# One shared score tile, head banks that alternate, and score products made half a step early in a decoder's joint stage

## The chip, the core and the metric

The kernel runs on one core of one Trainium2 chip. The metric is device time in microseconds (us), lower is better. The core has engines that run side by side, each with its own queue of instructions in a fixed order: PE (matrix products and, with an identity, transposes), DVE (vectors), ACT (activations such as exp), POOL (vectors too), and SP, which here starts transfers (DMA). They signal each other through semaphores. An instruction that waits holds up all that stands behind it on its engine. PE writes its products to PSUM, an on-chip memory[...], from which DVE and ACT read.

## The reference

Two decoder layers, each of self-attention, cross-attention and a feed-forward part, with a layer norm after each residual. The change lies in layer 0's cross-attention and the feed-forward part after it. Cut to these:

```python
x = _layernorm(x + _L0_attn_ref(x, ...))
x = _layernorm(x + _L0_xattn_ref(x, ctx_2048, ...))      # 16 heads of 16, 2048 rows, 2048 keys
x = _layernorm(x + _L0_ffn_ref(x, ...))
...
# in _L0_xattn_ref:
q = _fq_sym(q, axis=-1); k = _fq_sym(k, axis=-1); v = _fq_sym(v, axis=2)   # rounded to 8 bits
attn = softmax(einsum('bhqd,bhkd->bhqk', q, k))
attn = _fq_unsigned(attn, axis=-1)                                        # 0..255 per row
out = einsum('bhqk,bhkd->bhqd', attn, v)
# in _L0_ffn_ref:
h = silu(gate) * up
out = einsum('bsi,hi->bsh', h, w_down)
```

## The kernel before

The 2048 rows are 16 tiles of 128. Layer 0's cross-attention and its feed-forward part form one joint stage, from about 878 to 1875 us, in which the feed-forward work of earlier rows is laid between the attention work of later ones. It is a loop over 128 steps `(gp, i, u)`: eight groups `gp` of two row tiles, in each eight pairs of heads `i`, in each the two row tiles `u`. So a group is 16 steps. A step handles two heads (`hh` 0 and 1) of one row tile against all 2048 keys.

A step has two halves (`part`) of 1024 keys. In each half:

- `scores` (L781) makes four products on PE of 128 rows by 512 keys: for c = 0 and 1 (512 keys each), one per head. The two heads use the upper and lower 64 rows of the array. Each head's two products go to a tile `s` of two PSUM banks. The pool keeps two such tiles, so each half reuses the tiles of the half before.
- `scaled` (L794) makes one DVE pass per head, which scales the 1024 scores into `e` and carries the row's running maximum. Below, S1 is the pass of head 0 and S2 that of head 1.
- `words_T` (L829) transposes on PE the 8-bit weights of an earlier step (four products); `words_out` (L835) copies them out of PSUM, on DVE in the first half and on ACT in the second.
- `context` (L847) multiplies 8-bit weights by values, ten or twelve small products a half in three halves of four. They are split in two parts by `hh`.
- `weights8` (L813) is ACT's exponential over 2048 keys for one head of the step before, straight to 8 bits. At the end of a step `exponent` (L809) negates the maximum for it.
- `spread` (L841) is POOL's cast that puts the weights in the order `context` wants.

The order on PE, DVE, ACT and POOL is that in which the code records the instructions (`manual_schedule`); nothing reorders them. Besides the attention, `unit` (L1057) makes a gate or an up product of the feed-forward part (two products of 128 by 256), twice in eight of a group's 16 steps, and starts the load of a coming weight block on SP. `pair_work` (L1064), at the end of each half, makes the queries of later tiles, the attention's output product, the feed-forward part's down product and the transposes around them. `later` and `due` put off the DVE, ACT and POOL sides of these to named places of following halves.

In the first group there is no feed-forward work, in the second only gate and up products. After the last step a tail finishes the last rows: `ffn_gate` with tag "s" takes the two score tiles in turn for eight gate and up pairs, while ACT reads the tile of the pair before (`ffn_out`), and `ffn_down_psum` takes one for the down product.

PE's order in one half of before: four score products; transposes; put-off PE work; in the second half the unit; both parts of the contexts; then `pair_work`, which holds the first half's unit.

Of the kernel before, what the change touches and what calls it, by code (L numbers as in the profile page):

```python
# [18 lines left out]
F32 = mybir.dt.float32  # L19
# [8 lines left out]
P = 128  # L28
# [4 lines left out]
G = 512  # L33
# [15 lines left out]
def decoder(ctx: ExitStack, tc: tile.TileContext, w: dict, out: bass.AP):  # L49
    nc = tc.nc  # L50
# [538 lines left out]
    with ExitStack() as ph:  # L589
# [188 lines left out]
            ssum = stat.tile([P, 2, 16], F32, tag="ssum", name="ssum", bufs=3)  # L778
            groups[gp] = ([], ssum)

        def scores(gp, i, u, half, st):  # L781

            t = 2 * gp + u
            s = [ps.tile([P, 2, G], F32, tag="s", name="s", bufs=2) for _ in range(2)]
            for c in range(2):
                at = (2 * half + c) * G
                for hh in range(2):
                    r = slice(64 * hh, 64 * hh + 64)
                    nc.tensor.matmul(  # L789
                        s[hh][:, c, :], lhsT=qT[t % 4][r, i, :], rhs=kT[r, i, at : at + G], start=True, stop=True  # L790
                    )
            return s

        def scaled(gp, i, u, half, hh, st, s):  # L794

            nc.vector.tensor_scalar(  # L796
                st["e"][hh][:, half, :],
                s[hh].rearrange("p a b -> p (a b)"),
                qs[2 * gp + u][:, 2 * i + hh : 2 * i + hh + 1],
                None if half == 0 else st["mx"][:, 0, hh : hh + 1],  # L800
                ALU.mult,
                ALU.max,
                accum_out=st["mx"][:, half, hh : hh + 1],
            )
# [24 lines left out]
        def words_T(hh, st):  # L829
            pt = ps.tile([P, 4, P], F32, tag="tp", name="aTp", bufs=2)  # L830
            for b in range(4):
                nc.tensor.transpose(pt[:, b, :], st["a"][hh][:, b * P : (b + 1) * P], ident)  # L832
            return pt

        def words_out(hh, st, pt, copy):  # L835

            at = wk.tile([P, 4, P], F32, tag="at", name="at", bufs=3)
            copy(at.bitcast(U16), pt.bitcast(U16))  # L838
            st["at"][hh] = at
# [75 lines left out]
        def ffn_gate(q, i, n, tag="misc"):  # L915

            if n == 0:
                pp = ps.tile([P, 2, G] if tag == "s" else [P, 2, 2 * P], F32, tag=tag, name="gu", bufs=2 if tag == "s" else 1)
                ffn_ps[q] = pp[:, 0].rearrange("p (n c) -> p n c", n=2) if tag == "s" else pp
            at = slice((q % 2) * 2 * P, (q % 2) * 2 * P + 2 * P)  # L920
            wt = wgu[i, n]
            for k in range(2):
                nc.tensor.matmul(  # L923
                    ffn_ps[q][:, n, :], lhsT=wt[:, k, :], rhs=xT[q // 2][:, k, at], start=k == 0, stop=k == 1
                )
# [23 lines left out]
            eng.tensor_tensor(hs[q][:, i], th, gu[:, 0], ALU.mult)  # L949

        def ffn_down_psum(tag="misc"):
            pp = ps.tile([P, 2, G] if tag == "s" else [P, G], F32, tag=tag, name="pd", bufs=2 if tag == "s" else 1)
            return (pp[:, 0] if tag == "s" else pp).rearrange("p (u d) -> p u d", u=2)

        def ffn_down(q, js, pd):
            for j in js:
# [100 lines left out]
        def unit(n, k, at):  # L1057

            gp, r = n // 16, n % 16
            q = gp - 1 if r >= 8 else gp - 2  # L1060
            if r in units and 0 <= q < LAST:
                ffn_half(q, units[r], k, at)
# [52 lines left out]
        with tc.manual_schedule(engines=set(ordered)):  # L1115
            for n in range(len(steps) + 9):
                now = steps[n] if n < len(steps) else None
                if now is not None:
                    if n % 16 == 0:
                        group(n // 16)  # L1120
                    if n < NB:
                        nc.gpsimd.tensor_tensor(xs[n], xs[n], bp, ALU.add)
                    states[n] = {
                        "e": [wk.tile([P, 2, 2 * G], F32, tag="e", name="e", bufs=4) for _ in range(2)],
                        "mx": stat.tile([P, 2, 2], F32, tag="smx", name="smx"),
                        "a": [],
                        "at": {},
                    }
                for part in range(2):
                    at = 2 * n + part  # L1130
                    if now is not None:
                        s = scores(*now, part, states[n])
                        for hh in range(2):
                            scaled(*now, part, hh, states[n], s)
                    due(at, "DVE")

                    m = n - 2 + part
                    if 0 <= m < len(steps):
                        pt = words_T(1 - part, states[m])
                        words_out(1 - part, states[m], pt, nc.scalar.copy if part else nc.vector.tensor_copy)  # L1140
                    due(at, "PE")
                    if part == 1:
                        unit(n, 1, at)
                    for hh in range(2):

                        q = n - 3 if (n - 3) % 2 == 1 else n - 4
                        turn = (2 * (n - q) + part, hh)
                        if 0 <= q < len(steps) and turn in turns:
                            gp, i, _ = steps[q]
                            if turn == (7, 0) and i % 4 == 0:  # L1150
                                os[gp, i // 4] = ps.tile([P, 2 * P], F32, tag="o", name="o")
                            o = os[gp, i // 4]
                            context(i, range(*turns[turn]), aTs[gp, i], o)
                            if turn == (9, 1):
                                aTs.pop((gp, i))
                                if i % 4 == 3:
                                    later(
                                        at + 1,
                                        "ACT first",
                                        nc.scalar.copy,  # L1160
                                        ot[:, i // 4],
                                        os.pop((gp, i // 4)).rearrange("p (u q) -> p u q", u=2),
                                    )
                                if i == 7 and gp < LAST:
                                    later(at, "DVE last", sums, gp)
                                    for u in range(2):
                                        later(at + 1, "POOL", by_dim, gp, u)
                    due(at, "ACT first")

                    if 0 <= n - 1 < len(steps):  # L1170
                        weights8(*steps[n - 1], part, states[n - 1])
                    due(at, "ACT")
                    if 0 <= n - 2 < len(steps):
                        gp, i, u = steps[n - 2]
                        if part == 0 and u == 0:
                            aTs[gp, i] = wk.tile([P, NB, 2, 2 * P], BF16, tag="aT", name="aT")
                        due(at, "POOL first")
                        spread(u, part, states[n - 2], aTs[gp, i])
                    due(at, "POOL first")
                    due(at, "POOL")  # L1180
                    if now is not None and part == 1:
                        exponent(states[n])
                    due(at, "DVE last")
                    if (n, part) == (len(steps), 1):
                        later(at + 1, "DVE", sums, LAST)
                        for u in range(2):
                            later(at + 2, "POOL", by_dim, LAST, u)
                    if n < len(steps):
                        pair_work(n, bool(part))
                    else:  # L1190
                        tail_work(n, bool(part))
                if n == len(steps) + 3:
                    ffn_load_all()
                states.pop(n - 3, None)
            assert not put_off, put_off

            for i in range(NI):
                for n in range(2):
                    ffn_gate(LAST, i, n, "s")
                th, gu = ffn_tiles(LAST, i, tail=True)  # L1200
                ffn_out(LAST, th, gu)
                ffn_sigmoid(th, nc.vector)
                ffn_mult(LAST, i, th, gu, nc.vector)
            exp_tables()
            for u in range(2):
                ffn_put_out(LAST, range(NI * u, NI * u + NI), 0, "s")
                due(1, "DVE")
            due(1, "POOL")
            due(2, "POOL first")
# [498 lines left out]
```

## Time and profile before

| | |
|---|---|
| median of three runs | 2923.34 us (2921.56 to 2929.32) |
| the profiled execution, and its span | 2931.01 us, 2929.3 us |
| mean granted PE clock | 0.951 of full speed |
| busy over the span: PE, DVE, ACT, POOL | 2617.0, 1985.8, 1583.3, 1238.2 us |
| joint stage: first to last score pass | 879.6 to 1815.7 us |
| eight groups of it | 108.5, 112.9, 116.7, 119.5, 119.5, 119.5, 119.5, 120.1 us |
| busy 1340 to 1460: PE, DVE, ACT, POOL | 97.06, 97.91, 93.79, 83.95 of 120 us |

A line of a group of the profile has the source line, the engine and operation, the tile written and the tile read, shapes and count, then busy time in us and the mean of one in ns, and last the engine's idle time ahead of it and what ended most of that. A line of the timeline has the start and the length in us, engine, line, operation, tiles and count of records; brackets hold the idle time before it and who ended it. PE's 32-bit products appear as two records each. PEld is the loading of weights to PE. The granted clock is the share of full speed that PE was given.

### The profile page before, as it was taken

Reading aid. Unit: us, or ns where it says so; the run is one execution under the profiler, and the core shown is the slowest. Engines: PE = TensorE matmul, PEld = TensorE weight load, DVE = VectorE, ACT = ScalarE, POOL = GpSimd, SP = SyncE. Lnnn points to the kernel's source line nnn. Section 1 sums busy time; section 2 is a strip of 40 time slices with the busy share of each in tenths; the row PEclk is TensorE's granted clock in tenths of the full one; section 3 lists DMA queues with packets and bytes.
Section 4 is the critical chain, followed back from the end, with each engine's and each line's share of the span. In section 5 each row is a group of like instructions: output and inputs, shape, how many; then the busy total and the mean of one; then the engine's idle time right before and its main releaser. Section 6 shows DMA issues by size and latency. Waiting matters only on the chain. (4 is left out here: it accounts for less than half of the span.)

```text
span 2929.3 us, 43541 instructions
## 1 busy us (share of the span) xinstructions
PE 2617.0 (89%) x15989; PEld 1629.2 (56%) x16020; DVE 1985.8 (68%) x4501; ACT 1583.3 (54%) x2858; POOL 1238.2 (42%) x1390
## 2 busy tenths in 40 slices
PE   6999999999977778888787888899988899999998
PEld 3677777777743344444444444566655554655646
DVE  5677878777668888878878876377777764233232
ACT  3455555555536887878778777255555443122120
POOL 5544444444365666767768667322322210000000
PEclk9999999999986899989989898899999999999999
DMA  8000000000010000100000001310010012021110
GB/s 234 1 1 1 1 1 1 1 1 1 1 41 5 1 17 14 30 12 19 23 12 26 12 19 27 110 58 2 2 46 12 7 26 73 29 62 40 47 58 15
DMA packets 84997, 79.61 MB, mean 27 GB/s; under 512 B 19728, under 2 KB 66288, under 8 KB 84272
## 3 DMA queue, kind: packets, MB, share of 16 engines
q1 hardware_dynamic: 83520, 73.41, 8.2%
q0 software_dynamic: 1264, 3.42, 0.5%
q8 instruction: 126, 2.06, 0.3%
q14 instruction: 87, 0.71, 0.1%
HBM read 74.57 MB, written 2.23 MB: 26 GB/s over the span
## 5 line engine op out<-in xcount | busy, mean ns | idle before, releaser
L842 POOL CAST aT<-at 128x2048 bf16<-128x2048 uint8 x256 | 482.9, 1891 | 253.6 <-DVE at L838 221.4
L820 ACT ACTIVATE a<-e,snl 128x2048 uint8<-128x2048 f32 x256 | 513.4, 2005 | 2.8
L796 DVE TENSOR_SCALAR_CACHE_REDUCE e<-s,qs 128x1024 f32<-128x1024 f32 x256 | 319.0, 1282 | 123.9 <-PE s L789 110.6
L796 DVE TENSOR_SCALAR_CACHE_REDUCE e<-s,qs,smx 128x1024 f32<-128x1024 f32 x256 | 333.7, 1341 | 44.8 <-PE s L789 42.7
L832 PE MATMUL aTp<-ident,a 128*128 128x128 f32 x1024 | 191.5, 316 | 103.5 <-ACT a L820 103.1
L789 PE MATMUL s<-kT,qT 64*128 64x512 bf16 x1024 | 221.4, 427 | 49.2 <-DVE e L796 45.0
L832 PEld LDWEIGHTS aTp<-ident,a 128*128 128x128 f32 x1024 | 122.8, 156 | 243.1 <-ACT a L820 210.8
L838 ACT COPY at<-aTp 128x1024 uint16<-128x1024 uint16 x128 | 129.5, 1012 | 199.4 <-PE aTp L832 182.2
L1620 DVE TENSOR_TENSOR h<-h,up 128x512 f32<-128x512 f32 (+1 forms) x100 | 68.8, 688 | 192.6 <-PE up L1616 191.3
L1619 ACT ACTIVATE h<-gate 128x512 f32<-128x512 f32 (+1 forms) x100 | 59.7, 597 | 220.4 <-PE gate L1616 220.2
L1616 PE MATMUL gate<-xT,w_L_ffn_w1g 128*128 128x512 f32 x352 | 167.7, 595 | 0.0
L1616 PE MATMUL up<-xT,w_L_ffn_w1u 128*128 128x512 f32 x352 | 165.4, 592 | 0.0
L1330 DVE TENSOR_REDUCE amx<-sc 128x8 f32<-128x1024 f32 x96 | 116.8, 1216 | 65.1 <-PE sc L1321 64.8
L855 PE MATMUL o<-aT,vq 128*32 128x256 bf16 x2048 | 160.7, 294 | 0.0
L1647 PE MATMUL py<-w_L_ffn_w2T,h 128*128 128x256 f32 x704 | 154.6, 379 | 0.0
L1333 ACT ACTIVATE pr<-pr 128x1024 f32<-128x1024 f32 x96 | 101.6, 1059 | 89.1 <-DVE pr L1332 89.1
L1342 ACT COPY prT<-tp 128x512 f32<-128x512 f32 x192 | 104.3, 584 | 78.0 <-PE tp L1341 77.7
L1647 PEld LDWEIGHTS py<-w_L_ffn_w2T,h 128*128 128x128 f32 x704 | 133.7, 190 | 18.3
L789 PEld LDWEIGHTS <-qT 64*128 64x128 bf16 x1024 | 42.7, 96 | 161.9 <-issue 159.5
L443 ACT ACTIVATE pls<-sc,lm,rms_rs 128x128 f32<-128x128 f32 x256 | 113.8, 454 | 21.9 <-DVE lm L439 21.9
L373 PE MATMUL proj<-Wlk,xT 128*128 128x512 f32 x256 | 121.2, 595 | 3.9 <-DMA Wlk<-in_L_attn_Wlk 1.7
L923 PE MATMUL gu<-xT,wgu 128*128 128x256 f32 x448 | 122.3, 397 | 2.2 <-ACT gu_s L942 0.4
(319 smaller groups left out, 5905.5 us busy)
## 6 DMA issues: line engine op xcount, KB each, us to landing
wgu<-in_L_ffn_gu SPq DMA_DIRECT2D x112, 128.0 KB
sh<-share SPq DMA_DIRECT2D x32, 256.0 KB
sh<-share SPq DMA_DIRECT2D x16, 224.0 KB
sh<-share SPq DMA_DIRECT2D x16, 192.0 KB
w_L_ffn_w1g<-in_L_ffn_w1g SPq DMA_DIRECT2D x1, 2816.0 KB
w_L_ffn_w1u<-in_L_ffn_w1u SPq DMA_DIRECT2D x1, 2816.0 KB
w_L_ffn_w2T<-in_L_ffn_w2T SPq DMA_DIRECT2D x1, 2816.0 KB
sh<-share SPq DMA_DIRECT2D x16, 160.0 KB
```

What stands on the lines that cost most here:

```text
L373: nc.tensor.matmul(pp.rearrange("p h d -> p (h d)"), lhsT=xTt(b, k), rhs=wts[nm, hg][:, k, :], start=k == 0, stop=k == 1)
L789: nc.tensor.matmul(s[hh][:, c, :], lhsT=qT[t % 4][r, i, :], rhs=kT[r, i, at : at + G], start=True, stop=True)
L796: nc.vector.tensor_scalar(st["e"][hh][:, half, :], s[hh].rearrange("p a b -> p (a b)"), qs[2 * gp + u][:, 2 * i + hh : 2 * i + hh + 1], No ...
L820: nc.scalar.activation(a.bitcast(U8), st["e"][hh].rearrange("p a b -> p (a b)"), AF.Exp, bias=st["nm"][:, hh : hh + 1], accum_out=groups[g ...
L832: nc.tensor.transpose(pt[:, b, :], st["a"][hh][:, b * P : (b + 1) * P], ident)
L838: copy(at.bitcast(U16), pt.bitcast(U16))
L842: nc.gpsimd.tensor_copy(aT[:, :, hh, u * P : (u + 1) * P].rearrange("p (b j) q -> p b j q", j=4), st["at"].pop(hh).bitcast(U8).rearrange(" ...
L855: nc.tensor.matmul(o[r : r + 32], lhsT=vq[:, n, h // 2, h % 2 : h % 2 + 2].rearrange("p w d -> p (w d)"), rhs=aT[:, n, hh], start=n == 0 a ...
L923: nc.tensor.matmul(ffn_ps[q][:, n, :], lhsT=wt[:, k, :], rhs=xT[q // 2][:, k, at], start=k == 0, stop=k == 1)
L1330: nc.vector.tensor_reduce(mx, sc, AX.X, ALU.max)
L1616: nc.tensor.matmul(pp[:rows], lhsT=wt[:, k, :], rhs=xT[g][:, k, :], start=k == 0, stop=k == 1)
L1647: nc.tensor.matmul(py, lhsT=h[:rows, i4 * P : (i4 + 1) * P], rhs=wt, start=n == 0, stop=n == len(parts) - 1)
```

## The change

- The two score tiles become one tile `s4` of four banks, made once. `banks` picks a head's two: in a first half head 0 has banks 0 and 1 and head 1 has 2 and 3; in a second half head 0 has 0 and 2, head 1 has 1 and 3. So the two c = 0 products of each half go to the two banks that head 0 had in the half before.
- `scores` makes one c at a time. The c = 0 pair of the coming half is made in the half before, between the two parts of the contexts, right after the transposes. The c = 1 pair stays at the start of its half.
- The transposes move from ahead of the contexts to between their parts; the second half's unit moves from ahead of the contexts to behind them.
- On ACT and DVE, `words_out` moves behind the exponentials; so ACT's copy of the second half follows that half's exponential.
- The tail's gate, up and down products use parts of `s4`.

PE's order in one half of after: the c = 1 pair; put-off PE work; first part of the contexts; transposes; the coming half's c = 0 pair; second part of the contexts; in the second half the unit; then `pair_work`. The numbers of products, passes, exponentials and copies are the same.

```diff
-        def scores(gp, i, u, half, st):
+        s4 = ps.tile([P, 4, G], F32, name="s4")
+        def banks(half, hh):
+            return s4[:, 2 * hh : 2 * hh + 2] if half == 0 else s4[:, hh::2]
+        def scores(gp, i, u, half, c):
             t = 2 * gp + u
-            s = [ps.tile([P, 2, G], F32, tag="s", name="s", bufs=2) for _ in range(2)]
-            for c in range(2):
-                at = (2 * half + c) * G
-                for hh in range(2):
-                    r = slice(64 * hh, 64 * hh + 64)
-                    nc.tensor.matmul(
-                        s[hh][:, c, :], lhsT=qT[t % 4][r, i, :], rhs=kT[r, i, at : at + G], start=True, stop=True
-                    )
-            return s
+            at = (2 * half + c) * G
+            for hh in range(2):
+                r = slice(64 * hh, 64 * hh + 64)
+                nc.tensor.matmul(
+                    banks(half, hh)[:, c, :], lhsT=qT[t % 4][r, i, :], rhs=kT[r, i, at : at + G], start=True, stop=True
+                )
...
-                s[hh].rearrange("p a b -> p (a b)"),
+                banks(half, hh),
...
             if n == 0:
-                pp = ps.tile([P, 2, G] if tag == "s" else [P, 2, 2 * P], F32, tag=tag, name="gu", bufs=2 if tag == "s" else 1)
+                if tag == "s":
+                    pp = s4[:, 2 * (i % 2) : 2 * (i % 2) + 2]
+                else:
+                    pp = ps.tile([P, 2, 2 * P], F32, tag=tag, name="gu")
...
-                        s = scores(*now, part, states[n])
+                        if at == 0:
+                            scores(*now, 0, 0)
+                        scores(*now, part, 1)
                         for hh in range(2):
-                            scaled(*now, part, hh, states[n], s)
+                            scaled(*now, part, hh, states[n])
                     due(at, "DVE")
-
                     m = n - 2 + part
-                    if 0 <= m < len(steps):
-                        pt = words_T(1 - part, states[m])
-                        words_out(1 - part, states[m], pt, nc.scalar.copy if part else nc.vector.tensor_copy)
                     due(at, "PE")
-                    if part == 1:
-                        unit(n, 1, at)
                     for hh in range(2):
...
+                        if hh == 1 and 0 <= m < len(steps):
+                            pt = words_T(1 - part, states[m])
+                        if hh == 1 and at + 1 < 2 * len(steps):
+                            scores(*steps[(at + 1) // 2], (at + 1) % 2, 0)
...
+                    if part == 1:
+                        unit(n, 1, at)
                     due(at, "ACT first")
...
                         weights8(*steps[n - 1], part, states[n - 1])
+                    if 0 <= m < len(steps):
+                        words_out(1 - part, states[m], pt, nc.scalar.copy if part else nc.vector.tensor_copy)
                     due(at, "ACT")
```

## The prediction

> **What bounds the kernel now.** I read the page first, then the waits of the joint stage (880 to 1830 us), the stage's windows, and the timeline of one step. In the page's groups the two maximum passes on DVE (L796; S1 for the first head of a half, S2 for the second) are the stage's largest idle engine that waits for PE:
>
> ```profile
> L796 DVE TENSOR_SCALAR_CACHE_REDUCE e<-s,qs 128x1024 f32<-128x1024 f32 x256 | 319.0, 1282 | 123.9 <-PE s L789 110.6
> L796 DVE TENSOR_SCALAR_CACHE_REDUCE e<-s,qs,smx 128x1024 f32<-128x1024 f32 x256 | 333.7, 1341 | 44.8 <-PE s L789 42.7
> L789 PE MATMUL s<-kT,qT 64*128 64x512 bf16 x1024 | 221.4, 427 | 49.2 <-DVE e L796 45.0
> ```
>
> The waits (total us, times, longest) say the same in sum: DVE waits for scores, PE waits for DVE to free them, and PE's transposes wait for the exponentials.
>
> ```profile
> DVE e L796 <- PE s L789: 153.3, 161, 4.1
> PE aTp L832 <- ACT a L820: 103.1, 158, 1.6
> PE s L789 <- DVE e L796: 45.0, 70, 1.5
> ```
>
> The windows (length, then busy us and count of PE, PEld, DVE, ACT, POOL, granted clock, DMA) show a steady group of 16 steps in the last row: DVE works 97.9 of 120 us, no engine is full, and the loop DVE to PE to DVE sets the pace. The other rows are one stretch inside a group where the clock falls.
>
> ```profile
> 1249.00:1257.00 8.00, 6.47 (x50) 4.28 (x48) 6.32 (x13) 5.28 (x6) 3.73 (x2) 1.00 0.01 3
> 1257.00:1265.00 8.00, 5.67 (x34) 2.58 (x33) 6.00 (x11) 5.29 (x6) 4.82 (x8) 0.78 0.00 0
> 1265.00:1273.00 8.00, 7.38 (x42) 3.71 (x40) 5.26 (x9) 5.14 (x6) 5.06 (x3) 0.58 0.00 0
> 1340.00:1460.00 120.00, 97.06 (x655) 53.55 (x652) 97.91 (x166) 93.79 (x119) 83.95 (x79) 0.91 0.07 18
> ```
>
> From the starts of the S1 passes in the timeline, the eight groups take 108.5, 112.9, 116.7, then four times 119.5, and 120.1 us. Two half steps at clock 1.00 (start, length, engine, line):
>
> ```profile
> 1344.38 1.28 DVE L796 TENSOR_SCALAR_CACHE_REDUCE e<-s,qs 128x1024 f32<-128x1024 f32 x1 [1.63 <-PE s L789]
> ...
> 1345.59 1.28 DVE L796 TENSOR_SCALAR_CACHE_REDUCE e<-s,qs 128x1024 f32<-128x1024 f32 x1
> ...
> 1345.81 0.72 PE L855 MATMUL o<-aT,vq 128*32 128x256 bf16 x10
> 1346.46 1.13 PE L923 MATMUL gu<-xT,wgu 128*128 128x256 f32 x4
> ...
> 1346.79 0.68 DVE L838 COPY at<-aTp 128x1024 uint16<-128x1024 uint16 x1
> 1347.53 0.61 PE L789 MATMUL s<-kT,qT 64*128 64x512 bf16 x4
> 1348.17 1.34 DVE L796 TENSOR_SCALAR_CACHE_REDUCE e<-s,qs,smx 128x1024 f32<-128x1024 f32 x1 [0.69 <-PE s L789]
> ...
> 1349.44 1.34 DVE L796 TENSOR_SCALAR_CACHE_REDUCE e<-s,qs,smx 128x1024 f32<-128x1024 f32 x1
> 1349.75 0.72 PE L855 MATMUL o<-aT,vq 128*32 128x256 bf16 x10
> 1350.40 1.02 PE L789 MATMUL s<-kT,qT 64*128 64x512 bf16 x4
> 1351.37 1.28 DVE L796 TENSOR_SCALAR_CACHE_REDUCE e<-s,qs 128x1024 f32<-128x1024 f32 x1 [0.58 <-PE s L789]
> ```
>
> See that the contexts (L855) and the gate product (L923) run while DVE does S1 and S2. Only the score products lie between S2 and the next S1: S2 ends at 1349.44 + 1.34 = 1350.78, S1 starts at 1351.37, a gap of 0.59.
>
> **The step that decides: what the early products wait for.** In the built program of the changed kernel, the first early product (c = 0) of a half waits for S2 of the half before, in all 255 halves that have one, and the later products (c = 1) wait for nothing. S1 waits for the last of the four products, S2 for no product. So the waits are kept for the one tile `s4`, not for its banks. Before, with a tile per head, the first head's product waited for S1 only, and S1 waited for its own head's two products. So the banks that S1 frees can't be refilled while S2 runs. Worse, PE is in order: behind the early pair stand the second part of the contexts, the unit of the next stage (L923), query, output and down products, and only then the pair that S1 needs. All of that moves from beside the passes to the gap between S2 and S1. DVE, and behind it the exponentials and POOL, wait for it.
>
> **Cost of a gap, full clock.** From the rows above:
> - Base 0.9 us: the 0.59 of today, plus 0.22 for a second pair (four products take 0.61, one has a median of 0.386), plus some 0.1 for changing between kinds of products (the first score to the transposes behind it: 0.54 for two pairs of 0.22).
> - Second part of the contexts, six products: ten take 1346.46 - 1345.81 = 0.65, so 0.39. It is in 24 of the 32 gaps of a group (from the turns).
> - A gate or up unit: 1347.53 - 1346.46 = 1.07. Sixteen in a steady group.
> - Query twice and output twice, each two products of the unit's shape: 4 x 1.07 = 4.3. Down, 16 products; four take 1.99 in the timeline, so 8.0. Three sets of four transposes at 0.63: 1.9.
>
> S1 start to S2 end is 1.21 + 1.28 = 2.49 in the first half, 1.27 + 1.34 = 2.61 in the second; 16 steps of both make 81.6. A steady group is 81.6 + 32 x 0.9 + 24 x 0.39 + 16 x 1.07 + 4.3 + 8.0 + 1.9 = 151 us, against 119.5.
>
> **The clock, where a rule and the trace part.** The Trainium skill, "TensorE: Matmul & The Clock Gate", section "Why this matters for your kernels", asks for no PE gaps longer than about 3 us and then promises no drop. In the changed kernel PE stands idle some 1 us per half (2.5 us of passes less 0.5 for c = 1, 0.4 of contexts and 0.65 of transposes), so by the rule the clock stays full: 151. But in the rows at 1257 and 1265 the clock is 0.78 and 0.58 with no PE wait over 1.9 us. There DVE and PE take turns too, at PE busy x clock of 0.55; the changed group has about 97 x 0.91 / 160, the same 0.55. I take the trace, between that stretch (mean 0.68) and the group's mean of 0.91: clock 0.8. Of the gaps' 69 us all but 0.36 us per gap of fixed latency (11.5) scale, so 58 x 0.25 = +14.5: 165.5.
>
> **The sum.** Groups 2 to 6: 5 x 165.5 less 594.7 = +233. Group 7 has no queries (-2.7): 163 against 120.1, +43. Group 0 has only contexts and queries in the gaps: 81.6 + 28.8 + 8.6 + 2.1 + clock 7 = 128 against 108.5, +20. Group 1, ten units, no down products: 136 + 11 = 147 against 112.9, +34. That is +330.
>
> **The other parts.** The tail's eight gate units used two score tiles in turn; now each waits for ACT's copy of the one before, again because of the one tile. PE ran 64 gate products without a break (16.18 us); now it waits each time for a tanh of 0.38 that overlaps a copy of 0.58, about 1.0 with the start: eight handovers, +8. The exponentials ahead of the copies: a copy on ACT (1.01) and the POOL spread behind it come up to 2.0 us later in the second half. Contexts of a pair start a full step after its last spread, so that is hidden as long as a step lasts over 6 us; exposed it would cost 1 us a step, 128 us; it may also gain up to the 103 us for which PE's transposes waited for exponentials, were PE still bound there. With DVE's new gaps neither is last: I take 0. The passes' two-bank access in the second half: the nearest row is L796 itself, 1.28 and 1.34 for 1024 elements; a penalty of a bank change each pass would be under 0.1 (512 x 0.1 = 50 us), a gain nil as it reads as many elements. I take 0. DVE's copy (0.68) and its late adds lie in the gaps beside PE's work; they were partly exposed before, which the group times carry. No DMA is added; the weight loads of the next stage are issued at the same steps by SP, and their 10 us to landing is not last.
>
> Profiled: span 2929.3, execution 2931.0. 2931 + 330 + 8 = 3269. The median shown is 2923.3, 7.7 below that execution; so 3261, say 3260.
>
> **Rivals.**
> 1. The clock stays full, as the rule has it: five groups +160, group 7 +29, group 0 +13, group 1 +23, tail +8, together +233: 3157. For it: PE is never idle over 1.2 us. Against it: the rows at 1257 and 1265.
> 2. The clock falls to 0.65 through the stage: 58 x 0.54 = 31 on 151, so 182 a group: +316, +59, +28, +46, +8 = +457: 3380. For it: the same rows. Against: at the lower clock PE is busy for longer, and the stage of before comes back to 1.00 each time.
> 3. Not slower: the early pair does run beside S2. It decides whether that pair waits for S1's end or S2's; with S1's, PE has S2's 1.3 us for the pair, contexts and unit (0.32 + 0.39 + 1.07 = 1.78), so a gap is 0.6 in light halves and 1.0 with a unit, of which DVE's copy covers one in two. That is about 16 us idle a group, where DVE now idles 119.5 - 97.9 = 21.6: -5.7 x 7 = -40, so 2883. The profile's 153 us of waiting speak for room; the built program's waits speak against it.
> 4. A milder serial loss: full clock, and the base of 0.9 is too high by 0.3, as c = 0 and c = 1 run closer than I take it (32 x 0.3 x 8 = 77): 3157 - 77 = 3080.
>
> **How the numbers follow.** Forecast 3260: 0.50. Rival 1: 0.20. Rival 2: 0.16. Rival 4: 0.09. Rival 3: 0.03, and some 0.02 for a change that comes out even. The range from 3120 to 3400 takes in forecast and rivals 1 and 2 with their spread, and the lesser bound of bank access. About 0.3% is what a measurement of this kernel can tell from no change; faster 0.03, same 0.02, slower 0.95.
>
> **What would show it.** In the changed profile: DVE waiting for scores for some 350 to 450 us instead of 153, before S1 only, almost never before S2; PE's first early product released by DVE in most halves; L796 still 1.28 and 1.34; a steady group of 150 to 180 us; the stage's clock below 0.91. PE waits for the exponentials should nearly vanish. Gate products in the tail should show waits for ACT. A group under 125 us, or early products that start while S2 runs, would prove the deciding step wrong; a group near 151 with clock near 1, only the clock's term.

## The result, and the profile after

| | before | after |
|---|---|---|
| median (runs) | 2926.33 us (2921.56 to 2931.52, 4) | 3342.18 us (3329.80 to 3347.70, 4) |
| profiled execution, its span | 2931.01, 2929.3 us | 3337.07, 3335.4 us |
| granted PE clock, whole span | 0.951 | 0.882 |
| eight groups of the joint stage | 108.5, 112.9, 116.7, 4 x 119.5, 120.1 us | 134.9, 157.1, 173.7, 176.8, 172.1, 177.7, 173.0, 169.0 us |

The ratio is 1.1415, 95% interval 1.1372 to 1.1457: 14% slower. The profiled executions differ by 406 us, of which the eight groups hold 398. (The groups' times run from the first S1 of each to that of the next, the last to the end of the last S2.)

The score pass and product groups of the page after (busy us, mean ns, then the idle time before them and who ended it):

```profile
L794 PE MATMUL s<-kT,qT 64*128 64x512 bf16 x1024 | 250.8, 493 | 392.5 <-DVE e L800 391.2
...
L800 DVE TENSOR_SCALAR_CACHE_REDUCE e<-s,qs 128x1024 f32<-128x1024 f32 x256 | 318.5, 1281 | 321.8 <-PE s L794 225.0
L800 DVE TENSOR_SCALAR_CACHE_REDUCE e<-s,qs,smx 128x1024 f32<-128x1024 f32 x256 | 334.0, 1342 | 240.7 <-PE s L794 240.7
...
L836 PE MATMUL aTp<-ident,a 128*128 128x128 f32 x1024 | 217.8, 349 | 0.8 <-ACT a L824 0.8
```

The passes take as long as before (1282 and 1341 ns there), so reading two banks that are not neighbours, as the second half now does, costs nothing. What grew is the idle time ahead of them: 123.9 + 44.8 = 169 us before, 321.8 + 240.7 = 563 us now. The waits of the stage (total us, times, longest) show both directions of it:

```profile
DVE e L800 <- PE s L794: 465.7, 213, 4.2
PE s L794 <- DVE e L800: 391.2, 252, 2.8
```

PE waited for DVE 70 times before, 45 us in all; now 252 times, in nearly all of the 255 halves, 391 us. The transposes' wait for exponentials is gone: 0.8 us in all, where it was 103.1. One turn at the lower clock, from the timeline:

```profile
1627.05 1.34 DVE L800 TENSOR_SCALAR_CACHE_REDUCE e<-s,qs,smx 128x1024 f32<-128x1024 f32 x1
...
1628.45 0.39 PE L794 MATMUL s<-kT,qT 64*128 64x512 bf16 x2 [1.80 <-DVE e L800]
1628.78 0.69 PE L859 MATMUL o<-aT,vq 128*32 128x256 bf16 x6
1629.39 2.07 PE L930 MATMUL gu<-xT,wgu 128*128 128x256 f32 x4
1631.39 0.61 PE L794 MATMUL s<-kT,qT 64*128 64x512 bf16 x2
...
1632.14 1.28 DVE L800 TENSOR_SCALAR_CACHE_REDUCE e<-s,qs 128x1024 f32<-128x1024 f32 x1 [3.75 <-PE s L794]
```

S2 ends at 1627.05 + 1.34 = 1628.39. Only then does the early pair start (1628.45), after PE has stood idle for 1.80 us. Behind it come the six contexts and the unit, which takes 2.07 here against 1.13 at full clock, then the c = 1 pair, then S1: a gap of 3.75 us where the kernel before had 0.59. The windows show the clock (the figure right behind the five engines' busy times) in the first two groups and in two steady ones:

```profile
881.00:1016.00 135.00, 88.44 (x464) 39.81 (x463) 92.27 (x149) 82.01 (x94) 66.60 (x50) 0.58 0.00 1
1016.00:1173.00 157.00, 112.83 (x593) 54.40 (x592) 95.87 (x159) 92.29 (x111) 75.82 (x61) 0.67 0.03 8
...
1524.00:1696.00 172.00, 121.21 (x652) 63.80 (x652) 97.72 (x165) 94.86 (x118) 84.18 (x79) 0.78 0.05 13
1696.00:1874.00 178.00, 126.47 (x652) 66.45 (x652) 98.19 (x165) 95.31 (x120) 84.62 (x80) 0.75 0.04 13
```

DVE's busy time per group is what it was (98 us); a steady group lasts 175 us in place of 119.5. The clock is lowest just where it costs most: in the turn above it is 1.00 during the two passes (1625.79 to 1628.39) and 0.58 in the gap behind them (1628.39 to 1632.14). Over the 160 gaps of the five steady groups it is 0.70 in the mean, beside their passes 0.84.

### The profile page after: what moved, and what is told of

Its sections match the earlier page's. It is cut to its first block, busy times and chain, and to the rows that moved or that the text cites. A ratio compares the mean times of both kernels' runs of the same rounds, so it can differ in the third digit from the quotient of the medians.

```text
span 3335.4 us, 43446 instructions
## 1 busy us (share of the span) xinstructions
PE 2816.2 (84%) x15989; PEld 1712.2 (51%) x16020; DVE 1989.3 (60%) x4501; ACT 1595.5 (48%) x2858; POOL 1241.8 (37%) x1390
## 5 line engine op out<-in xcount | busy, mean ns | idle before, releaser
L794 PE MATMUL s<-kT,qT 64*128 64x512 bf16 x1024 | 250.8, 493 | 392.5 <-DVE e L800 391.2
L800 DVE TENSOR_SCALAR_CACHE_REDUCE e<-s,qs 128x1024 f32<-128x1024 f32 x256 | 318.5, 1281 | 321.8 <-PE s L794 225.0
L800 DVE TENSOR_SCALAR_CACHE_REDUCE e<-s,qs,smx 128x1024 f32<-128x1024 f32 x256 | 334.0, 1342 | 240.7 <-PE s L794 240.7
L794 PEld LDWEIGHTS <-qT 64*128 64x128 bf16 x1024 | 72.3, 97 | 551.3 <-issue 551.0
L859 PE MATMUL o<-aT,vq 128*32 128x256 bf16 x2048 | 231.4, 340 | 0.0
L836 PE MATMUL aTp<-ident,a 128*128 128x128 f32 x1024 | 217.8, 349 | 0.8 <-ACT a L824 0.8
L836 PEld LDWEIGHTS aTp<-ident,a 128*128 128x128 f32 x1024 | 141.2, 175 | 84.7 <-issue 56.6
L930 PE MATMUL gu<-xT,wgu 128*128 128x256 f32 x448 | 181.1, 544 | 1.7 <-ACT gu_s L949 1.5
L1342 DVE TENSOR_REDUCE amx<-sc 128x8 f32<-128x1024 f32 x96 | 116.7, 1215 | 61.7 <-PE sc L1333 61.5
L859 PEld LDWEIGHTS <-vq 128*32 128x32 bf16 x2048 | 79.7, 106 | 137.0 <-issue 128.3
L1659 PEld LDWEIGHTS py<-w_L_ffn_w2T,h 128*128 128x128 f32 x704 | 133.7, 190 | 18.3
L930 PEld LDWEIGHTS gu<-xT,wgu 128*128 128x128 f32 x448 | 103.0, 254 | 46.7 <-issue 28.2
```

The costliest lines, as they stand in the source:

```text
L794: nc.tensor.matmul(banks(half, hh)[:, c, :], lhsT=qT[t % 4][r, i, :], rhs=kT[r, i, at : at + G], start=True, stop=True)
L800: nc.vector.tensor_scalar(st["e"][hh][:, half, :].rearrange("p (a b) -> p a b", a=2), banks(half, hh), qs[2 * gp + u][:, 2 * i + hh : 2 * ...
L859: nc.tensor.matmul(o[r : r + 32], lhsT=vq[:, n, h // 2, h % 2 : h % 2 + 2].rearrange("p w d -> p (w d)"), rhs=aT[:, n, hh], start=n == 0 a ...
L930: nc.tensor.matmul(ffn_ps[q][:, n, :], lhsT=wt[:, k, :], rhs=xT[q // 2][:, k, at], start=k == 0, stop=k == 1)
L1342: nc.vector.tensor_reduce(mx, sc, AX.X, ALU.max)
L1659: nc.tensor.matmul(py, lhsT=h[:rows, i4 * P : (i4 + 1) * P], rhs=wt, start=n == 0, stop=n == len(parts) - 1)
```

## The experiments

My theory: the waits of the one tile hold the early pair until S2 ends, PE's fixed order puts all that stands behind it into the gap between S2 and S1, and the clock, which falls with PE's idle stretches, makes that work longer. Rivals: the moved copies and exponentials; the order on PE or the one tile, without the early pair; a clock that is no cause. Each ratio is to runs of the kernel before that were taken beside that experiment.

| kernel | median us | ratio to before (95%) |
|---|---|---|
| e1 changed kernel, pair at the start of its half | 2921.79 | 0.9982 (0.9975 to 0.9989) |
| e2 before, exponentials first | 2858.87 | 0.9767 (0.9751 to 0.9782) |
| e3 changed kernel with filler products | 3163.48 | 1.0809 (1.0792 to 1.0826) |
| e4 four one-bank tiles, early pair | 2985.15 | 1.0198 (1.0181 to 1.0215) |
| e5 four one-bank tiles, no early pair | 3009.68 | 1.0280 (1.0264 to 1.0295) |
| e6 changed kernel, contexts ahead of the early pair | 3126.78 | 1.0682 (1.0666 to 1.0698) |
| e7 e2 with the changed order on PE | 2877.99 | 0.9828 (0.9811 to 0.9845) |
| e8 e2 with products by head | 2840.00 | 0.9703 (0.9687 to 0.9720) |
| e9 e6 with filler products | 3080.01 | 1.0521 (1.0495 to 1.0548) |
| e10 changed kernel, copies first | 3349.61 | 1.1428 (1.1379 to 1.1477) |

**e1, the pair back at the start of its half.**

```diff
-                        if at == 0:
-                            scores(*now, 0, 0)
+                        scores(*now, part, 0)
                         scores(*now, part, 1)
...
-                        if hh == 1 and at + 1 < 2 * len(steps):
-                            scores(*steps[(at + 1) // 2], (at + 1) % 2, 0)
```

> The changed kernel with one edit: the c = 0 pair is made at the start of its own half again, next to the c = 1 pair; the one tile, the order of transposes, contexts and unit, and the exponentials ahead of the copies stay. If the loss comes from PE work that stands between the early pair and the c = 1 pair (my theory), the gap is four products, about 0.8 us at full clock, against 0.59 of before: +0.2 us in half of the gaps, +0.1 in the rest, some +40 us, and the tail's +11: about 2975 us (2940 to 3020), stage clock near 0.9. If another part loses the time (the order of exponentials and copies, the moved transposes and units, the one tile itself), it stays above 3200.

Measured: 2921.79 us. Undoing the place of two products alone takes back all of the loss, 420 us. It came below the expected range. This kernel keeps the exponentials ahead of the copies, which alone turned out to be worth 67 us (e2), and 2975 - 67 would have been 2908; that this is the reason was not tested. Its waits:

```profile
PE s L794 <- DVE e L800: 170.5, 179, 2.8
DVE e L800 <- PE s L794: 124.8, 130, 4.1
```

PE still waits for S2 as the tile demands, but with no other work queued between the pairs; DVE's wait falls from 465.7 to 124.8 us.

**e2, the exponentials ahead of the copies, on the kernel before.**

```diff
                     if 0 <= m < len(steps):
                         pt = words_T(1 - part, states[m])
-                        words_out(1 - part, states[m], pt, nc.scalar.copy if part else nc.vector.tensor_copy)
...
                         weights8(*steps[n - 1], part, states[n - 1])
+                    if 0 <= m < len(steps):
+                        words_out(1 - part, states[m], pt, nc.scalar.copy if part else nc.vector.tensor_copy)
```

> The kernel before with one part of the change: words_out recorded behind the exponentials, on ACT and DVE. My theory: it has little to do with the loss, 2890 to 2940 us; a gain is possible because PE's transposes waited 103 us for exponentials. Rival (the exponentials ahead of the copies delay the copies and POOL, and that is the loss): over 3100 us.

Measured: 2858.87 us, 2.3% faster than before. The rival falls, and my neutral guess too: a steady group takes 109.1 to 111.8 us. Its waits of the stage, and its transposes:

```profile
PE s L789 <- DVE e L796: 104.5, 144, 1.5
DVE e L796 <- PE s L789: 97.3, 120, 4.1
...
L832 PE MATMUL aTp<-ident,a 128*128 128x128 f32 x1024 | 178.9, 300 | 1.4 <-ACT a L820 1.4
```

DVE waits 97.3 us for scores in place of 153.3, and the transposes' wait for exponentials falls from 103.1 us to 1.4. PE had been late with scores because its transposes, ahead of the next half's scores in order, waited for exponentials that stood behind a copy. The clock rose with it, from 0.91 to 0.98 in the last of the steady groups. The copies on ACT and on DVE were moved together; their shares were not separated.

**e3, filler products that keep PE busy.** Its four added products are overwritten by the transposes that follow; nothing of the output changes.

```diff
             pt = ps.tile([P, 4, P], F32, tag="tp", name="aTp", bufs=2)
+            for _ in range(4):
+                nc.tensor.matmul(pt.rearrange("p b q -> p (b q)"), lhsT=ident16, rhs=kT[:, 0, 0:G], start=True, stop=True)
```

> The changed kernel with four more products of 128 x 512 on PE ahead of each set of transposes, into the tile that the transposes then overwrite; they stand where PE idles beside the maximum passes, and their results are not used. If the fall of the clock to about 0.76 in the stage is caused by PE's idle stretches and makes up the part beyond the serial cost at full clock, the clock rises above 0.9 and the time falls to 3150 to 3230 us. If the clock is not set by PE's idleness, or does not price the gaps, the time stays at 3340 or grows by up to 0.9 us x 256 = 220 us.

Measured: 3163.48 us. 1024 more products on PE make the kernel 179 us faster. Two steady groups in its windows, and a turn of its timeline:

```profile
1440.00:1591.00 151.00, 118.86 (x783) 64.86 (x782) 98.00 (x165) 94.70 (x120) 84.61 (x79) 1.00 0.05 15
1591.00:1742.00 151.00, 118.84 (x783) 64.91 (x782) 97.98 (x165) 94.68 (x119) 84.58 (x79) 1.00 0.05 15
```

```profile
1450.04 1.28 DVE L800 TENSOR_SCALAR_CACHE_REDUCE e<-s,qs 128x1024 f32<-128x1024 f32 x1
...
1451.38 0.39 PE L794 MATMUL s<-kT,qT 64*128 64x512 bf16 x2 [0.96 <-DVE e L800]
1451.70 0.51 PE L861 MATMUL o<-aT,vq 128*32 128x256 bf16 x6
1452.14 1.13 PE L932 MATMUL gu<-xT,wgu 128*128 128x256 f32 x4
1453.20 0.39 PE L794 MATMUL s<-kT,qT 64*128 64x512 bf16 x2
...
1453.64 1.34 DVE L800 TENSOR_SCALAR_CACHE_REDUCE e<-s,qs,smx 128x1024 f32<-128x1024 f32 x1 [1.70 <-PE s L794]
```

The clock is 1.00 from the second group on (0.93 in the first), and the same chain of pair, contexts, unit, pair takes from S2's end (1450.04 + 1.28 = 1451.32) to 1453.64, 2.32 us. The groups take 121.0, 135.7, then about 151 each, and 146.6 us. So the loss in the groups has two parts: the serial chain at full clock, some 222 us over the groups of before, and the clock, about 176 us.

**e4 and e5, waits kept per bank.** Four tiles of one bank; a pass then takes one bank, so there are four a half.

```diff
-        s4 = ps.tile([P, 4, G], F32, name="s4")
-        def banks(half, hh):
-            return s4[:, 2 * hh : 2 * hh + 2] if half == 0 else s4[:, hh::2]
+        sb = [ps.tile([P, G], F32, name=f"sb{b}") for b in range(4)]
+        def bank(half, hh, c):
+            return sb[2 * hh + c] if half == 0 else sb[hh + 2 * c]
...
+            for c in range(2):
+                k = 2 * half + c
                 nc.vector.tensor_scalar(
+                    st["e"][hh][:, half, c * G : (c + 1) * G],
+                    bank(half, hh, c),
...
+                    None if k == 0 else st["mx"][:, k - 1, hh : hh + 1],
...
+                    accum_out=st["mx"][:, k, hh : hh + 1],
```

> The changed kernel with four one-bank tiles in place of the one of four banks, so waits are kept per bank; a maximum pass must then take one bank, 512 scores, four passes a half instead of two. The early pair is kept. Cost: each pass has some fixed time, by the 1.28 us of 1024 scores and about one score a ns that is 0.2 us, so +0.4 us a half, +100 us if exposed. If the one tile's waits are the cause, the early pair now runs while head 1's passes run, the gaps nearly vanish, and the time is below the one of before plus the passes' cost: 2800 to 2950 us. If the position of the work on PE alone were the cause, whatever the waits, it stays above 3200.

> The kernel with four one-bank tiles and four passes a half, but with both pairs made at the start of their half. It is the like-for-like partner of the one with the early pair (2985 us). If the early pair is worth something once waits are per bank, this one is slower by the gaps it saves, up to 0.4 us a half, 3000 to 3080 us. If DVE's four passes are the bound in both (it was busy 108 of 120 us), the two agree within 1%: 2960 to 3010 us.

Measured: 2985.15 us with the early pair, 3009.68 without (e5 adds e1's edit). With waits per bank, the early pair in the place that the changed kernel gives it gains 24 us; with the one tile the same place costs 420. That is the test of the deciding step. Neither beats the kernel before: the passes of e4, from the groups of its stage,

```profile
L802 DVE TENSOR_SCALAR_CACHE_REDUCE e<-sb,qs,smx 128x512 f32<-128x512 f32 x768 | 611.2, 808 | 95.1 <-PE sb L794 38.2 <-DVE e L802 0.5
...
L802 DVE TENSOR_SCALAR_CACHE_REDUCE e<-sb,qs 128x512 f32<-128x512 f32 x255 | 188.6, 740 | 0.1
```

are 611 + 189 = 800 us in place of 319 + 334 = 653, and DVE, busy 108 of 120 us, is nearly full. Its wait for PE's scores is down to 38 us. I had put e4 at 2800 to 2950. The 0.2 us of fixed time per pass that I allowed holds for a pass without a carried maximum: 512 scores more take 1.28 - 0.74 = 0.54 us, which leaves 0.74 - 0.54 = 0.20. But each pass that was added also carries a maximum, 0.07 us more: two passes cost 0.74 + 0.81 - 1.28 = 0.27 us more than one, some 140 us in all and not 100.

**e6 and e9, what stands behind the early pair.** Both context parts go ahead of the transposes, the pair behind them; e9 adds e3's filler.

```diff
-                        if hh == 1 and 0 <= m < len(steps):
-                            pt = words_T(1 - part, states[m])
-                        if hh == 1 and at + 1 < 2 * len(steps):
-                            scores(*steps[(at + 1) // 2], (at + 1) % 2, 0)
...
+                    if 0 <= m < len(steps):
+                        pt = words_T(1 - part, states[m])
+                    if at + 1 < 2 * len(steps):
+                        scores(*steps[(at + 1) // 2], (at + 1) % 2, 0)
                     if part == 1:
                         unit(n, 1, at)
```

> The changed kernel with both parts of the contexts ahead of the transposes, so that the early pair stands behind them and only the unit and the other products are left between it and the c = 1 pair. My theory: six context products leave 187 gaps; 0.39 us each at full clock, 0.51 at 0.77: -73 to -95 us, 3250 us (3210 to 3285), the DVE gap in light halves 1.1 instead of 1.7. If PE's idle stretch beside the passes is too short to take them, or the order within PE does not matter, it stays at 3340.

> Both context parts ahead of the early pair (3127 us), plus the four unused products of the filler ahead of the transposes. It says how much of the 215 us between that kernel and the changed one is the six products' place and how much the clock that came with it. At full clock the place is worth 0.39 us x 24 gaps x 8 groups = 75 us less than the changed kernel with the filler (3163): 3090 us (3075 to 3110), with clock 1.00 in the stage. If the place is worth far more for another reason, under 3050; if the filler's 1 us no longer fits beside the passes, over 3130.

Measured: e6 3126.78 us, 215 less than the changed kernel, where I had expected about 90 less; e9 3080.01, as expected. At full clock, with the filler in both, taking six products out of the gap is worth 3163 - 3080 = 83 us. The other 132 us of e6 came with the clock, as a steady stretch of its windows shows:

```profile
1285.00:1435.00 150.00, 103.71 (x659) 60.28 (x658) 99.95 (x169) 97.30 (x121) 84.53 (x79) 0.90 0.05 15
```

The same for e9:

```profile
1289.00:1440.00 151.00, 124.24 (x829) 71.47 (x828) 103.78 (x174) 100.22 (x127) 90.53 (x85) 1.00 0.05 15
```

0.90 in e6, where the changed kernel has 0.76. Less work in the gap brings a higher clock, and the clock shortens what is left of the gap.

**e7, the order on PE alone.** e2 with the changed kernel's transposes and unit in their new places, two tiles and no early pair.

```diff
-                    if 0 <= m < len(steps):
-                        pt = words_T(1 - part, states[m])
                     due(at, "PE")
-                    if part == 1:
-                        unit(n, 1, at)
...
+                        if hh == 1 and 0 <= m < len(steps):
+                            pt = words_T(1 - part, states[m])
...
+                    if part == 1:
+                        unit(n, 1, at)
                     due(at, "ACT first")
```

> The kernel with exponentials ahead of copies and two score tiles (2859 us), plus the changed kernel's order on PE: transposes between the contexts' parts, unit behind them. It splits the 63 us between that kernel and the one with the pair at the start of its half. If the one tile costs them (0.2 us more gap in each half, 256 x 0.2 = 50, and the tail's 11), this one stays at 2855 to 2875 us. If the order on PE does, it comes to 2900 to 2925 us.

Measured: 2877.99 us, between the two forecasts: the order costs 19 us, and the one tile, without the early pair, 2922 - 2878 = 44 us (32 in the eight groups, the rest mainly in the tail).

**e8, a version that beats both.** With the tiles of before, head 0's two products need only S1's end. They are recorded first.

```diff
-            for c in range(2):
-                at = (2 * half + c) * G
-                for hh in range(2):
-                    r = slice(64 * hh, 64 * hh + 64)
+            for hh in range(2):
+                r = slice(64 * hh, 64 * hh + 64)
+                for c in range(2):
+                    at = (2 * half + c) * G
```

> The kernel with exponentials ahead of copies and two score tiles, with the four products of a half in another order: both of head 0, then both of head 1. Head 0's two wait only for S1, so they can be made while S2 runs, and S1 of the next half finds them ready: the gap of 0.59 us goes, in light steps 6.2 us become 5.6 to 5.8. Against it, the two heads' products no longer run side by side on the upper and lower rows: +0.22 us a pair, +0.43 us a half on PE, which is exposed where PE is late anyway. If the theory of who waits for whom holds: 2790 to 2840 us. If the loss of pairing outweighs it: 2870 to 2930 us.

Measured: 2840.00 us, 3.0% under the kernel before and 19 us under e2; just at the upper end of what I expected. A turn of its timeline:

```profile
1345.41 1.34 DVE L796 TENSOR_SCALAR_CACHE_REDUCE e<-s,qs,smx 128x1024 f32<-128x1024 f32 x1
1346.02 0.60 PE L789 MATMUL s<-kT,qT 64*128 64x512 bf16 x2
...
1346.76 1.28 DVE L796 TENSOR_SCALAR_CACHE_REDUCE e<-s,qs 128x1024 f32<-128x1024 f32 x1
...
1346.81 0.59 PE L789 MATMUL s<-kT,qT 64*128 64x512 bf16 x2 [0.19 <-DVE e L796]
```

Head 0's two products run while S2 does (1345.41 to 1346.75), and the next S1 starts at 1346.76: no gap. This is what the change was after, with nothing queued between. In groups 0 and 1 light steps fall from 6.2 to 5.5 us. In the later groups they take 5.9 to 6.0, and the heavy steps stay above 8 us; in some of these PE waits 1.5 to 1.9 us for DVE's adds (L891). So the gain stays small: groups 0 and 1 give 16 of the 19 us over e2, and groups 3 to 6, at a clock of 0.94 in place of 0.97, give nothing (441 us against 439).

**e10, the copies first again, in the changed kernel.**

```diff
+                    if 0 <= m < len(steps):
+                        words_out(1 - part, states[m], pt, nc.scalar.copy if part else nc.vector.tensor_copy)
                     due(at, "ACT first")
...
                         weights8(*steps[n - 1], part, states[n - 1])
-                    if 0 <= m < len(steps):
-                        words_out(1 - part, states[m], pt, nc.scalar.copy if part else nc.vector.tensor_copy)
```

> The changed kernel with the copies recorded ahead of the exponentials again, as before. Alone, on the kernel before, the exponentials ahead of the copies gained 67 us; the prediction took 0 for them in the changed kernel, since with its longer halves PE hardly waits for exponentials (0.8 us in all). If that holds, 3325 to 3360 us. If the gain is in the changed kernel too, and its loss of the other parts is so much larger, about 3400 us.

Measured: 3349.61 us, the same as the changed kernel within its spread. The 67 us of e2 are not there: with the copies first, in halves this long, the transposes wait 14.5 us for exponentials, against 103.1 in the kernel before.

## Why the prediction was right in kind and short by 80 us

The time forecast was 3260, the measured one 3342. Of these 82 us, 68 lie in the eight groups; the tail is within 2 us of its forecast, and most of the rest comes from the profiled execution, which lay 7.7 us above the median before and lies 5.1 below it after. In the steps of the prediction:

- **The deciding step held.** The early pair waits for S2. e1 (its place undone, -420 us) and e4 beside e5 (waits per bank, the same place -24 us) show it. So the rival that ends not slower was ruled out by the waits of the built program, not by the profile: with waits per bank the early pair did gain.
- **The price of the gap held.** Pair, contexts, unit, pair: forecast 0.9 + 0.39 + 1.07 = 2.36 us, in e3 2.32. At full clock the groups were forecast at 121 (128 less its clock term of 7), 136, 151 and 149 us; e3 has 121.0 (at 0.93), 135.7, 151 and 146.6. Its passes take 81.6 us a steady group and its gaps 69.4, as forecast. By what lies in a gap: with contexts alone 1.28 to 1.35 us (1.29 forecast), with a unit 1.88 (1.97), with both 2.3 to 2.4 (2.36). Only the few gaps with nothing between the pairs were off, 0.71 for 0.9. Rival 1, the changed kernel at full clock, stood at 3157; e3 measures 3163.
- **The clock term was too small.** This is the step that failed. I took 0.8 for steady groups and a term of 14.5 us each; steady groups take 174.7 us in the mean, 23.7 over the 151.0 of e3. Groups 0 and 1 fell to 0.58 and 0.67: 13.9 and 21.4 us in place of 7 and 11. Over all groups the clock cost 176 us, where I had 105, and the difference is nearly all of the miss in the groups (398 against 330). The value for the stage was not far off: the trace has 0.74 to 0.78, and at 0.76 the same formula, 58 x (1/0.76 - 1), gives 18.3 us, not 23.7. What was wrong is that one clock was taken for the whole group. The work that is exposed stands in the gaps, and there the clock is 0.70; 58 x (1/0.70 - 1) = 24.9. The stretch at 1257 to 1273 of the kernel before, with a mean of 0.68, was the better guide; half way to the group's mean was a compromise for which no row spoke.
- **PE's idle stretch was put too low.** I took 1 us per half, with 0.5 of the c = 1 pair beside the passes. But S1 waits for that pair, so it ends ahead of the passes: without it the same sum gives 1.45, and the trace has 391.2 / 252 = 1.55.
- **The rule that was weighed.** The Trainium skill ("TensorE: Matmul & The Clock Gate", section "Why this matters for your kernels") asks, against drops of throughput within a kernel, for no PE gaps over some 3 us. In the stage of the changed kernel no idle stretch of PE is longer than 2.8 us, and the waits for DVE are 1.55 in the mean, yet the clock was 0.76. The measurement decides: here shorter waits, one in every half, were enough.
- **Exponentials ahead of copies at 0** held in the changed kernel (e10), though alone they gain 67 us (e2). The forecast gave the reason: with the new gaps DVE, and not the exponentials, is waited for.
- **The tail** was put at +8. It has the waits:

```profile
2252.74 3.78 PE L930 MATMUL s<-xT,wgu_all 128*128 128x256 f32 x8 [0.95 <-ACT gu_t L949]
...
2260.42 1.99 PE L930 MATMUL s<-xT,wgu_all 128*128 128x256 f32 x8 [0.95 <-ACT gu_t L949]
```

  There are eight of about 1.0 us each, and the first two units, 3.78 us in place of 1.99, add 3.6, which I had not forecast. Other steps gave about 5 us back, half of it ahead of the first of these units. From the last S2 to the end of the kernel it is 1120.2 against 1113.6, +7, so the agreement with +8 is in part luck.
- DVE's wait for scores was forecast at 350 to 450 us; it is 465.7. At the clock of e3 it is 297.7, so the excess too is a matter of clock.

What stays open is how the clock is set. e3 and e6 show that it follows what PE does in the stage: more work in PE's idle stretch raises it, and so does less work in the gap. But PE's busy share alone does not decide it. Over groups 2 to 6 PE is busy for 79% of the time in e3 at a clock of 1.00, for 83% in e5 at 0.89 and for 69% in e6 at 0.90; the full-speed work in that time, share times clock, gives no order either (0.79, 0.74, 0.63). A stretch of e5, to set beside those of e3 and e6 above:

```profile
1340.00:1460.00 120.00, 102.66 (x592) 49.87 (x590) 102.62 (x265) 86.28 (x106) 74.24 (x71) 0.85 0.06 16
```

Nor does the mean wait for DVE decide it: 103.5 / 235 = 0.44 us in e5, and 262.6 / 253 = 1.04 us in e3.

## What to carry to other kernels

Before moving work ahead, look up in the built program what the moved instruction waits for: a part of a tile may wait as if it were the whole tile, and on an engine with a fixed order an early instruction that waits makes all behind it late. Making something early pays where what it needs is free early (e8: head 0's products need only S1), and only in steps where nothing else holds the next pass back (e8 gained in groups 0 and 1, not in groups 3 to 6). And a stage that alternates between PE and another engine pays for its gaps twice, in idle time and in clock; a first estimate at full clock is then a lower bound. For the price of the clock, take it in the gaps, not its mean over the stage.

## What the runs showed of the hardware that was not expected

- Adding work made it faster: 4 more products of 128 x 512 ahead of each of 256 sets of transposes brought the clock of the steady groups from 0.76 to 1.00 and the time from 3342 to 3163 us.
- The clock feeds back: six small products fewer in the gap were worth 83 us at a clock of 1.00, but 215 us where the clock could rise with them, from 0.76 to 0.90.
- The mean clock of a stage hides where it falls: with 0.76 in the steady groups it was 0.84 beside the passes and 0.70 in the gaps.
- A maximum pass over 512 scores took 0.74 us, or 0.81 with a carried maximum, against 1.28 and 1.34 for 1024.
